# Second norm, third norm and keys of a two-layer cross-attention kernel: the turning of 22 tiles moved from TensorE to DMA block moves and a VectorE 32x32 transpose

## Chip, cores and metric

The kernel runs on one core of a Trainium2 chip, as a single launch. The metric is device microseconds of that core from one launch, the median over several runs. Three runs of the kernel before are known: 907.7, 908.37 and 908.4 us, median 908.37 us. The profile is of one execution and counts from the first to the last instruction of the program; its span is 907.1 us.

The engines are named as the profile names them: PE (TensorE, matrix products), PEld (its weight loads), DVE (VectorE), ACT (ScalarE), POOL (GpSimd) and SP (SyncE, which here only issues DMAs).

## What is computed

Eight batches of a 128x512 token tile `x` go through two layers. Each layer is a gated cross-attention and then a gated dense layer, each on a layernorm of `x` and each added to `x`:

```python
x = x + tanh(g_xattn[0]) * L0_xattn(layernorm(x), ctx, mask, ...)   # 32 heads of 128
x = x + tanh(g_ffn[0])   * L0_ffn(layernorm(x), ...)                # 512x512, dequantized
x = x + tanh(g_xattn[1]) * L1_xattn(layernorm(x), ctx, ...)         # one head of 512
x = x + tanh(g_ffn[1])   * L1_ffn(layernorm(x), ...)                # dense, router, LoRA experts
```

The later stages, which the change touches, are the last three lines. `L1_xattn` is

```python
features_n = rmsnorm(features, fn_w)
Q = rmsnorm(text @ Wq.T + bq, qn_w)
K = rmsnorm(features_n @ Wk.T + bk, kn_w)
attended = softmax(Q @ K.T / sqrt(512)) @ features_n
```

## The kernel before

The first 780 us or so compute the first attention, with 32 heads. They are not touched. What follows are the later stages, for the eight batches `b` = 0 to 7, each a tile with 128 tokens on the partitions and 512 features along the free dimension. A product over features needs the features on the partitions, so each tile that enters a product is turned first.

The later stages are generators, one for each batch and kind of work:

- `ffn0(b)`: layernorm "h1", then the dense product `psf` (12 matmuls of 512 columns), added to `x` by DVE at L777. POOL has added the bias to `x` before that (L1172), so L777 waits for POOL too.
- `keys(b)`: DVE writes `k` (L1196, two halves), ACT squares it for the norm (L1182), POOL makes the inverse root (L421, L426), ACT scales it (L1208), PE turns it (L1127, tile `tpk`), DVE multiplies it by the norm weights into `kT` (L1211).
- `xattn1(b)`: layernorm "h2", the product `psq` (12 matmuls), `q` (DVE, L1233), its norm, the turn of `q` on PE (`tpq`), the scores `s` (four matmuls, eight rows of 128 columns in the trace, L1243), the softmax, a turn of the probabilities (`tpp`), and the product `av` added to `x` at L777.
- `ffn1(b)`: layernorm "h3", the product `o` in two halves of 328 columns (12 matmuls each), the router on DVE, the LoRA turn `thw`, the product `lb`, and the store to `out`.

All three layernorms are `layernorm(b, name)`. ACT makes minus the mean (L1143) and subtracts it (L1150). After a `yield`, `transposed()` turns the result with four 128x128 PE transposes into one PSUM tile `tph` (L1127). `parts_of()` then calls `split()`: ACT rounds the turned tile to the upper part of an fp32r pair (L169) and DVE subtracts that for the lower part (L170). ACT squares `x` for the variance (L1157) and POOL makes the inverse root. Every product is three matmuls for each block of 128 features (`product`, L178, L179, L182): high x high, high x low of the right side, low of the left side x high. So the third matmul of a product, some 0.46 us after the first, is the first that reads the lower part.

`pipeline(starts)` orders the work: in each of its steps, newly started generators advance first, then the older ones, each up to its next `yield`. `starts` gives the step in which each begins: `ffn0(b)` in step 1+b, `keys(b)` in step 4+b, `xattn1(b)` in step 9+b, `ffn1(b)` in step 17+b. Only PE is held to that order (`in_order(*ORD)`, with `ORD` the PE alone). For the other engines and for SP a scheduler decides the order when the program is built; on the chip each engine then takes its instructions strictly in that order and waits for each in turn.

Tiles live in a fixed number of buffers for each tag (`TAGS`): "page" 14, "raw" 7, "moved" 2, "pT" 2, "wo" 8. PSUM banks: "mm" 3 (for `psf`, `psq`, `av`, `o`, `lb`), "sc" 2, "av" 3.

The same detour that the change uses stands already in the first attention: `store_probs` writes the probabilities to DRAM (L725), `move_probs` reads them back in four DMAs so that the 32-row blocks change places (L732), and `transpose_probs` turns all 32x32 blocks with one DVE instruction (L741).

Of the kernel before, what the change touches and what calls it, by code (L numbers as in the profile page):

```python
# [8 lines left out]
F32 = mybir.dt.float32  # L9
# [18 lines left out]
Q32 = 32  # L28
NQ = P // Q32
# [10 lines left out]
OUT_LAG = 6  # L40
FIRST = 6
SHORT = 12
QUAD = 4
AHEAD = 3
WARMING = 7
# [21 lines left out]
def kernel(  # L67
# [37 lines left out]
    nc = tc.nc  # L105
# [3 lines left out]
    dram = ctx.enter_context(tc.tile_pool(name="dram", bufs=2, space=bass.MemoryType.DRAM))  # L109
# [13 lines left out]
    def wide_row(tag, name, dtype=F32):  # L123
        return slot([P, D], tag, name, dtype)
# [4 lines left out]
    def wide(t):  # L129

        return t.bitcast(F32)
# [36 lines left out]
    def split(high, low, src, low_engine=None):  # L168
        mark("high", nc.scalar.copy(high, src))  # L169
        mark("low", (low_engine or nc.vector).tensor_tensor(low, src, wide(high), ALU.subtract))  # L170
# [226 lines left out]
    xs = [keep([P, D], f"x{b}") for b in range(NB)]  # L397
# [31 lines left out]
    def over_free(w, n=P):  # L429

        return w.unsqueeze(2).to_broadcast([P, NDC, n])
# [201 lines left out]
    def by_block(t):  # L633

        return t.rearrange("p b (n k) -> p n b k", k=Q32)
# [315 lines left out]
    rows = []  # L951
# [170 lines left out]
    qkn = keep([P, NDC], "qkn")  # L1122
    def transposed(b, name, src):
        tag = "sc" if b % 2 and name in SC_NAMES else "av"
        tp = ptile([P, NDC, P], tag, f"tp{name}_{b}")
        for dc in range(NDC):
            nc.tensor.transpose(tp[:, dc, :], src[:, bass.ts(dc, P)], ident)  # L1127
        return tp

    def work(b, name, tag, shape=(P, D), dtype=F32):  # L1130
        return slot(list(shape), tag, f"{name}_{b}", dtype)

    def parts_of(b, name, src):

        t = work(b, name, "page", (P, NDC, 2, P), F32R)
        split(t[:, :, 0, :], t[:, :, 1, :], src)
        return t

    def layernorm(b, name, gate=None):


        negm = col(f"nm{name}", b)
        nc.scalar.mul(negm, col(f"sum{name}", b), -1.0 / D)  # L1143
        t = work(b, name, "wo")
        src, dst = xs[b], t
        if name == "h1":

            dst = t.rearrange("p (jj a r) -> p r a jj", jj=NDC, a=2)
            src = src.rearrange("p (r a jj) -> p r a jj", a=2, jj=NDC)
        nc.scalar.activation(dst, src, AF.Identity, bias=negm)  # L1150
        yield
        tp = transposed(b, name, t)
        if name == "h3" and b > 2:
            turns.pop(b - 3)()
        hT = parts_of(b, f"{name}T", tp)
        ss = col(f"ss{name}", b)
        nc.scalar.activation(  # L1157
            work(b, f"junk{name}", "raw"), xs[b], AF.Square, bias=negm, accum_out=ss
        )
        r = col(f"r{name}", b)  # L1160
        inverse_root(r, ss, 1e-5)
        rg = r
        if gate is not None:
            rg = col(f"rg{name}", b)
            nc.gpsimd.tensor_tensor(rg, r, gate, ALU.mult)
        yield
        return hT, r, rg
# [9 lines left out]
        return ps  # L1177

    def inverse_rms(b, name, src):
        junk = work(b, f"junk{name}", "raw")  # L1180
        ss = col(f"ss{name}", b)
        mark("rms", nc.scalar.activation(junk, src, AF.Square, accum_out=ss))  # L1182
        r = col(f"ir{name}", b)
        inverse_root(r, ss, 1e-6)
        return r

    kTs = [page([P, NDC, HALF, P], f"kT{i}", F32) for i in range(2)]
    fns = {}

    def keys(b):  # L1190
        half, j = divmod(b, HALF)
        k = work(b, "k", "v")
# [12 lines left out]
        r2 = inverse_rms(b, "k", k)  # L1205
        yield
        with behind("high"):
            nc.scalar.activation(k, k, AF.Copy, scale=r2)  # L1208
        yield
        tp = transposed(b, "k", k)  # L1210
        nc.vector.tensor_tensor(kTs[half][:, :, j, :], tp, over_free(qkn), ALU.mult)  # L1211
        yield

    def values(b):
# [168 lines left out]
    def ffn1_weights():  # L1383
        for dc in range(NDC):
            t = page([P, 2, 2, NS], f"bw{dc}")
            nc.sync.dma_start(out=wide(t).rearrange("p a h n -> p a (h n)"), in_=bw_kept[:, dc])
            for half in range(2):
                bw[dc, half] = [t[:, part, half] for part in range(2)]
        t = page([P, 2, D], "lora")
        nc.sync.dma_start(out=wide(t), in_=lora_kept)  # L1390
# [13 lines left out]
        nc.vector.tensor_scalar_mul(twice, twice, 2.0)  # L1404
        yield

    def ending():
# [38 lines left out]
        yield  # L1446

    key, ffn, att, last = ([s(b) for b in range(NB)] for s in (keys, ffn0, xattn1, ffn1))

    starts = [[ending()], ffn[:1], ffn[1:2], ffn[2:3], [ffn[3], key[0]]]  # L1450
    starts += [[ffn[b], key[b - 3]] for b in range(4, NB)]
    starts += [[att[0], key[5]], [att[1], key[6]], [att[2], key[7]]] + [[c] for c in att[3:] + last]
    starts[6].append(query_weights())
    starts[13].append(ffn1_weights())
    with in_order(*ORD):
        pipeline(starts)

# [71 lines left out]
```

## Time and profile before

| what | value |
|---|---|
| runs | 907.7, 908.37, 908.4 us |
| span of the profiled execution | 907.1 us |
| PE busy | 900.8 us (99%) |
| DVE busy | 673.1 us (74%) |
| ACT busy | 503.0 us (55%) |
| POOL busy | 460.3 us (51%) |
| granted TensorE clock, 40 slices | full in all of them |
| first product of `ffn0`, first of `psq`, first of `o` | 786.2, 820.5, 858.8 us |
| last PE turn of an "h3" tile | 890.2 us |

The profiled execution's own time on the clock of the runs is not listed beside its span; the three runs lie 0.6 to 1.3 us above the span, which is what lies before its first and after its last instruction.

How to read the profile: a group is a source line, engine and operation, `out<-in` by the program's names with buffer numbers left out, so `tph` stands for the turned tiles of all three norms. "Idle before" is time in which that engine waited, with what ended the wait. In a timeline the columns are the start, the duration, and the instruction; matmuls overlap, so what PE can deliver is read from start to start: 0.23 us for 512 columns, 0.11 us for a 128x128 transpose. A DMA row has the queue's issue time in the timeline, and its time to landing in the DMA view.

### The profile page before, as it was taken

To read this page: it belongs to the slowest core of one execution; us is meant where nothing else is said; L and a number is where in the kernel's file an instruction comes from. 1 tells how busy PE (TensorE), PEld (TensorE's weight loads), DVE (VectorE), ACT (ScalarE), POOL (GpSimd) and SP (SyncE) were. 2 spreads that over 40 slices of the span, in tenths; PEclk is the share of its full clock that TensorE was granted. 3 is DMA by queue.
4 is the path that set the end of the run, shared out by engine and by line. 5 is a ranking of instruction groups with operands and counts; after the bars stand their busy time and mean duration, and the time that the engine had idled before them with its cause. 6 is when DMAs were issued, how large, how long until landed. Compare 5 with 4: busy or idle time off the path is not lost.

```text
span 907.1 us, 16427 instructions
## 1 busy us (share of the span) xinstructions
PE 900.8 (99%) x5381; PEld 799.2 (88%) x5381; DVE 673.1 (74%) x1353; ACT 503.0 (55%) x1426; POOL 460.3 (51%) x513
## 2 busy tenths in 40 slices
PE   9999999999999999999999999999999999999998
PEld 7888888888888899999999999999999998888897
DVE  7888878789889866777677667666686877565587
ACT  6666555667555545545536445453454544588862
POOL 2355534114322436756747657583866844265441
PEclk9999999999999999999999999999999999999999
DMA  7755477889875956667574765766767566814001
GB/s 256 255 162 163 152 205 232 294 280 285 275 238 204 298 196 186 182 193 221 163 238 151 203 215 153 222 176 201 215 165 208 180 178 177 306 47 143 1 24 71
DMA packets 125223, 174.99 MB, mean 193 GB/s; under 512 B 17105, under 2 KB 54737, under 8 KB 124113
## 3 DMA queue, kind: packets, MB, share of 16 engines
q1 hardware_dynamic: 124992, 173.68, 61.5%
q8 instruction: 42, 0.69, 0.3%
q14 instruction: 45, 0.36, 0.1%
q10 hardware_dynamic: 144, 0.26, 0.1%
HBM read 109.86 MB, written 64.03 MB: 192 GB/s over the span
## 4 chain that ended last, share of the span: by engine, by line
PE 93%; DVE 3%; DMA 2%; ACT 1%; issue 0%; POOL 0%; SPq 0%; DVEq 0%; ACTq 0%; POOLq 0%
PE c_v L178 7%; PE c_v L179 6%; PE c_v L182 6%; PE pso L182 6%; PE pso L178 6%; PE pso L179 6%; PE sc L692 6%; PE av L756 6%; PE c_q L178 6%; PE c_q L179 6%; PE c_q L182 6%; PE c_k L178 4%; PE c_k L179 4%; PE c_k L182 4%; PE tph L1127 1%; DMA cxraw<-in_cxT_dram 1%
## 5 line engine op out<-in xcount | busy, mean ns | idle before, releaser
L709 ACT ACTIVATE s<-s,nm 128x128 f32<-128x128 f32 x256 | 99.8, 392 | 78.8 <-DVE nm L699 54.8
L777 DVE SCALAR_TENSOR_TENSOR x<-pso,tg,x 128x512 f32<-128x512 f32 x128 | 93.4, 741 | 52.2 <-PE pso L182 51.3
L717 POOL TENSOR_TENSOR s<-s,rs 128x512 f32<-128x512 f32 x64 | 66.7, 1042 | 111.1 <-DVE rs L715 63.2
L178 PE MATMUL pso<-wo_h,a 128*128 128x512 f32 x256 | 101.9, 411 | 0.0
L179 PE MATMUL pso<-wo_l,a 128*128 128x512 f32 x256 | 101.5, 397 | 0.0
L182 PE MATMUL pso<-wo_h,a 128*128 128x512 f32 x256 | 101.0, 395 | 0.1
L178 PE MATMUL c_v<-wvP,cxT 128*128 128x256 f32 x288 | 84.8, 294 | 0.2 <-ACT v L253 0.2
L182 PE MATMUL c_v<-wvP,cxT 128*128 128x256 f32 x288 | 81.4, 283 | 0.0
L179 PE MATMUL c_v<-wvP,cxT 128*128 128x256 f32 x288 | 81.4, 283 | 0.0
L757 ACT CAST a<-av 128x512 fp32r<-128x512 f32 x64 | 37.4, 584 | 74.4 <-PE av L756 74.0
L679 POOL TENSOR_TENSOR s<-mneg,bias 128x512 f32<-128x512 bf16 x64 | 75.9, 1186 | 0.1
L756 PE MATMUL av<-pT,v 128*128 128x128 f32 x512 | 71.2, 274 | 0.0
L756 PEld LDWEIGHTS av<-pT,v 128*128 128x128 f32 x512 | 67.1, 191 | 2.8
L692 PE MATMUL sc<-k,q 128*128 128x128 f32 x464 | 65.8, 274 | 0.0
L692 PEld LDWEIGHTS sc<-k,q 128*128 128x128 f32 x464 | 61.9, 191 | 3.2
L178 PE MATMUL c_v<-wvP,cxB 128*128 128x256 f32 x216 | 62.1, 289 | 0.0
L758 DVE TENSOR_TENSOR a<-av,a 128x512 fp32r<-128x512 f32 x64 | 43.4, 679 | 24.9 <-ACT a L757 24.5
L179 PE MATMUL c_v<-wvP,cxB 128*128 128x256 f32 x216 | 61.2, 283 | 0.0
L182 PE MATMUL c_v<-wvP,cxB 128*128 128x256 f32 x216 | 61.1, 283 | 0.0
L170 POOL TENSOR_TENSOR wo_l<-raw_wo,wo_h 128x512 fp32r<-128x512 f32 x32 | 41.4, 1293 | 33.8 <-ACT wo_h L169 33.8
L182 PEld LDWEIGHTS pso<-wo_h,a 128*128 128x128 f32 x256 | 48.2, 188 | 10.8 <-DVE a L758 1.3
L695 DVE TENSOR_TENSOR s<-sc,s 128x512 f32<-128x512 f32 x64 | 43.7, 683 | 17.1 <-PE sc L692 12.4
(277 smaller groups left out, 2808.4 us busy)
## 6 DMA issues: line engine op xcount, KB each, us to landing
keys<-keys SPq DMA_DIRECT2D x64, 256.0 KB, 3.5
queries<-queries SPq DMA_DIRECT2D x64, 256.0 KB, 3.5
through<-s SPq DMA_DIRECT2D x64, 256.0 KB, 2.6
moved<-through SPq DMA_DIRECT2D x256, 64.0 KB, 3.0
q<-queries SPq DMA_DIRECT2D x58, 256.0 KB, 3.8
k<-keys SPq DMA_DIRECT2D x58, 256.0 KB, 4.3
raw_wq<-in_wq_dram SPq DMA_DIRECT2D x32, 256.0 KB, 3.9
raw_wv<-in_wv_dram SPq DMA_DIRECT2D x32, 256.0 KB, 4.9
```

The lines of the kernel that those rows point to most:

```text
L170: mark("low", (low_engine or nc.vector).tensor_tensor(low, src, wide(high), ALU.subtract))
L178: nc.tensor.matmul(out, lhsT=lh, rhs=rh, start=first, stop=False, **more)
L179: nc.tensor.matmul(out, lhsT=lh, rhs=rl, start=False, stop=False, **more)
L182: nc.tensor.matmul(out, lhsT=ll, rhs=rh, start=False, stop=last, **more),
L679: nc.gpsimd.tensor_tensor(s, mneg[:, half], bias.unsqueeze(2).to_broadcast([P, NQ, HALF, Q32]), ALU.add)
L692: nc.tensor.matmul(ps[:, j, :], lhsT=q[:, cols], rhs=k[:, cols], start=True, stop=True)
L695: nc.vector.tensor_tensor(s, by_block(ps), s, ALU.add)
L709: e = nc.scalar.activation(one, one, AF.Exp, bias=nm[:, j : j + 1], accum_out=sm[:, j : j + 1])
L717: mark(f"norm{u}", nc.gpsimd.tensor_tensor(s, s, factors, ALU.mult))
L756: nc.tensor.matmul(av[:, b, :], lhsT=v[:, cols], rhs=pT[:, b, :], start=True, stop=True)
L758: mark("al", nc.vector.tensor_tensor(al, av, wide(ah), ALU.subtract))
L777: "x", nc.vector.scalar_tensor_tensor(xs[b], ps, factor, xs[b], ALU.mult, ALU.add, **out)
```

## The change

For the second norm ("h2", all eight batches), the third ("h3", batches 2 to 7) and the keys (all eight), the four PE transposes go: 22 tiles. In their place:

- ACT writes the normed tile in another order of its columns (`by_rows`), so that each quarter of a row has the pieces of all four feature blocks.
- `send()` issues one DMA that stores the tile to DRAM and four that read it back with 32-row blocks exchanged, all on SP's queue.
- `turned()` is one DVE transpose of 32x32 blocks, SBUF to SBUF.
- For these norms `split()` gets POOL for the lower part instead of DVE, and the multiplication of the keys by the norm weights goes from DVE to POOL as well.
- `xattn1(b)` begins two steps earlier, and "h2" waits two steps more between `send` and `turned`; the keys wait one step more. "h3" has no step more.
- The tile that takes the unused squares is one for all (`junk`) instead of one of "raw" for each.
- The loads of the weights of `ffn1` begin two steps later, and are issued only after the last `send` before them.

```diff
+    def send(b, name, t, tag):
+        through = dram.tile([P, NQ, NDC * Q32], F32, tag="rows", name=f"rows_{name}_{b}", bufs=6)
+        nc.sync.dma_start(out=through, in_=t.rearrange("p (n f) -> p n f", n=NQ))
+        moved = work(b, f"{name}moved", tag, (P, NQ, NDC, Q32))
+        blocks = through.rearrange("(i q) n f -> n q i f", q=Q32)
+        for j in range(NQ):
+            move = nc.sync.dma_start(
+                out=moved[bass.ts(j, Q32)].rearrange("p i b k -> p i (b k)"), in_=blocks[j]
+            )
+        mark("sent", move)
+        return moved
+    def turned(b, name, moved, tag):
+        t = work(b, f"{name}turned", tag, (P, NDC, P))
+        nc.vector.transpose(by_block(t), moved)
+        return t
...
+        far = name == "h2" or (name == "h3" and b >= FAR)
...
         nc.scalar.activation(dst, src, AF.Identity, bias=negm)
-        yield
-        tp = transposed(b, name, t)
+        if far:
+            moved = send(b, name, t, "raw")
+        yield
+        for _ in range(2 * (name == "h2")):
+            yield
+        if far:
+            tp = turned(b, name, moved, "raw")
+        else:
+            tp = transposed(b, name, t)
...
-        hT = parts_of(b, f"{name}T", tp)
+        hT = parts_of(b, f"{name}T", tp, nc.gpsimd if far else None)
...
-            nc.scalar.activation(k, k, AF.Copy, scale=r2)
-        yield
-        tp = transposed(b, "k", k)
-        nc.vector.tensor_tensor(kTs[half][:, :, j, :], tp, over_free(qkn), ALU.mult)
+            nc.scalar.activation(
+                by_rows(rows), k.rearrange("p (dc n k) -> p dc n k", n=NQ, dc=NDC), AF.Copy, scale=r2
+            )
+        moved = send(b, "k", rows, "moved")
+        yield
+        yield
+        t = turned(b, "k", moved, "pT")
+        nc.gpsimd.tensor_tensor(kTs[half][:, :, j, :], t, over_free(qkn), ALU.mult)
...
-    starts += [[att[0], key[5]], [att[1], key[6]], [att[2], key[7]]] + [[c] for c in att[3:] + last]
+    starts += [[key[b]] for b in range(5, NB)] + [[] for _ in range(5)] + [[c] for c in last]
+    for b in range(NB):
+        starts[7 + b].insert(0, att[b])
     starts[6].append(query_weights())
-    starts[13].append(ffn1_weights())
+    starts[15].append(ffn1_weights())
```

More of the change, by code (lines that the diff above doesn't have):

```diff
@@ L42 @@
 SHORT = 12
+FAR = 2
 QUAD = 4
@@ L1131, in work, with parts_of, by_rows @@
         return slot(list(shape), tag, f"{name}_{b}", dtype)
-    def parts_of(b, name, src):
+    def parts_of(b, name, src, low_engine=None):
         t = work(b, name, "page", (P, NDC, 2, P), F32R)
-        split(t[:, :, 0, :], t[:, :, 1, :], src)
+        split(t[:, :, 0, :], t[:, :, 1, :], src, low_engine)
+        return t
+    junk = wide_row("kq", "junk")
+    def by_rows(t):
+        return t.rearrange("p (n dc k) -> p dc n k", n=NQ, dc=NDC)
+    def send(b, name, t, tag):
[12 more added lines that the diff above has]
+        nc.vector.transpose(by_block(t), moved)
         return t
@@ L1149, in layernorm @@
             src = src.rearrange("p (r a jj) -> p r a jj", a=2, jj=NDC)
+        far = name == "h2" or (name == "h3" and b >= FAR)
+        if far:
+            dst = by_rows(t)
+            src = src.rearrange("p (dc n k) -> p dc n k", n=NQ, dc=NDC)
         nc.scalar.activation(dst, src, AF.Identity, bias=negm)
+        if far:
+            moved = send(b, name, t, "raw")
         yield
-        tp = transposed(b, name, t)
+        for _ in range(2 * (name == "h2")):
+            yield
+        if far:
+            tp = turned(b, name, moved, "raw")
+        else:
+            tp = transposed(b, name, t)
         if name == "h3" and b > 2:
             turns.pop(b - 3)()
-        hT = parts_of(b, f"{name}T", tp)
+        hT = parts_of(b, f"{name}T", tp, nc.gpsimd if far else None)
         ss = col(f"ss{name}", b)
         nc.scalar.activation(
-            work(b, f"junk{name}", "raw"), xs[b], AF.Square, bias=negm, accum_out=ss
+            junk, xs[b], AF.Square, bias=negm, accum_out=ss
         )
@@ L1179, in inverse_rms @@
     def inverse_rms(b, name, src):
-        junk = work(b, f"junk{name}", "raw")
         ss = col(f"ss{name}", b)
@@ L1206, in keys @@
         yield
+        rows = work(b, "krows", "v")
         with behind("high"):
-            nc.scalar.activation(k, k, AF.Copy, scale=r2)
+            nc.scalar.activation(
+                by_rows(rows), k.rearrange("p (dc n k) -> p dc n k", n=NQ, dc=NDC), AF.Copy, scale=r2
+            )
+        moved = send(b, "k", rows, "moved")
         yield
-        tp = transposed(b, "k", k)
-        nc.vector.tensor_tensor(kTs[half][:, :, j, :], tp, over_free(qkn), ALU.mult)
+        yield
+        t = turned(b, "k", moved, "pT")
+        nc.gpsimd.tensor_tensor(kTs[half][:, :, j, :], t, over_free(qkn), ALU.mult)
         yield
@@ L1385, in ffn1_weights @@
             t = page([P, 2, 2, NS], f"bw{dc}")
-            nc.sync.dma_start(out=wide(t).rearrange("p a h n -> p a (h n)"), in_=bw_kept[:, dc])
+            with behind("sent"):
+                nc.sync.dma_start(out=wide(t).rearrange("p a h n -> p a (h n)"), in_=bw_kept[:, dc])
             for half in range(2):
@@ L1389, in ffn1_weights @@
         t = page([P, 2, D], "lora")
-        nc.sync.dma_start(out=wide(t), in_=lora_kept)
+        with behind("sent"):
+            nc.sync.dma_start(out=wide(t), in_=lora_kept)
         lora.extend(t[:, part] for part in range(2))
```

## Prediction

> **What bounds the kernel.** First the page's busy shares and its chain of work that ended last:
>
> ```profile
> PE 900.8 (99%) x5381; PEld 799.2 (88%) x5381; DVE 673.1 (74%) x1353; ACT 503.0 (55%) x1426; POOL 460.3 (51%) x513
> PE 93%; DVE 3%; DMA 2%; ACT 1%; issue 0%; POOL 0%; SPq 0%; DVEq 0%; ACTq 0%; POOLq 0%
> ```
>
> PE is the path, and the waits of PE after 765 us add up to 0.2 us. So what leaves PE counts fully, and so does any wait that PE gets. The chain in order of time shows one step of the stage that the change meets first:
>
> ```profile
> 816.24 0.44 PE tpk L1127 x4
> 816.68 0.44 PE tph L1127 x4
> 817.12 0.23 PE psf L178
> ...
> 819.88 0.44 PE tpk L1127 x4
> ```
>
> A step is 3.64 us: two turns and twelve matmuls (2.85 us). Next, who else is near full in it. The windows give POOL 18.02 us of the 20 from 800 to 820, and POOL's timeline shows one whole cycle without a gap over 0.1 us:
>
> ```profile
> 810.25 0.19 POOL L1165 TENSOR_TENSOR cols<-cols,tg 128x1 f32<-128x1 f32 x1
> 810.52 0.19 POOL L421 TENSOR_SCALAR cols<-cols 128x1 f32<-128x1 f32 x1
> 810.79 0.55 POOL L426 TENSOR_TENSOR cols<-cols,neghalf 128x1 f32<-128x1 f32 x1
> 811.42 0.50 POOL L421 TENSOR_SCALAR cols<-cols 128x1 f32<-128x1 f32 x1
> 812.00 0.55 POOL L426 TENSOR_TENSOR cols<-cols,neghalf 128x1 f32<-128x1 f32 x1
> 812.52 1.43 POOL L1172 TENSOR_TENSOR x<-x,bias 128x256 f32<-128x256 f32 x2
> ```
>
> The cycle ends at 813.91: 3.66 us; the shortest (803.61 to 807.02) is 3.41. I take 3.45. POOL just keeps up with a PE step of 3.65, not with a shorter one.
>
> **What goes.** From start to start, a turned key takes PE 0.43 to 0.44 us, a turned "h2" 0.35 or 0.36, a turned "h3" 0.44 (the first 0.35): 8 x 0.435 + 8 x 0.355 + 2.55 = 8.9 us. Nothing hides it: **−8.9**. If nothing else changed, 908.4 would become 899.5.
>
> **What comes.** 22 DVE transposes (0.65 from start to start, L741) for 22 DVE instructions of 0.68 that move to POOL: DVE is even. POOL gets 14 lower parts at 1.29 (L170, `wo_l`) and 8 key products at 1.04 (L336, a 128x512 product with a broadcast column): 26 us more, 18 of them before the last `psq`. SP gets 22 x 5 = 110 DMAs. What one costs:
>
> ```profile
> 738.17 0.32 SPq L725 DMA_DIRECT2D through<-s  x1
> 738.59 1.82 SPq L732 DMA_DIRECT2D moved<-through  x4
> ...
> moved<-through SPq DMA_DIRECT2D x44, 64.0 KB, 2.2
> out_dram<-x SPq DMA_DIRECT2D x7, 256.0 KB, 2.0
> ```
>
> Four moves hold the queue 1.82 us, 0.455 each; a store lands 2.0 us after its issue, a move 2.2. So one tile costs SP 2.25 us, and a batch's key and "h2" together 4.5, against PE steps of 3.2 to 4.2.
>
> The order in which the changed program lists each engine's instructions decides the rest, since each engine takes its list strictly. I work with batch numbers and put durations from the rows on that list.
>
> *psf_7.* Without the key, a PE step is 0.355 + 2.845 = 3.20; the turn of batch 2 starts at 796.04 as before, so psf_6 would end at 815.25 (the last matmul drains till 815.45). POOL starts its first cycle at about 799 (the square of key 0, 1 us earlier than before); the bias of batch 6 is the fifth cycle's: 799.0 + 4 x 3.45 + 3.2 = 816.0. DVE before took the lower part of `h1T` of batch 7 ahead of that batch 6 addition:
>
> ```profile
> 816.06 0.68 DVE L170 TENSOR_TENSOR h1T<-tph,h1T 128x512 fp32r<-128x512 f32 x1
> 817.65 0.75 DVE L777 SCALAR_TENSOR_TENSOR x<-psf,cols,x 128x512 f32<-128x512 f32 x1 [0.91 <-POOL x L1172]
> ```
>
> In the changed list it stands behind it: x_6 (816.0, pitch 0.67), the transpose of key 0 (0.65), k_6 (0.80), then this lower part (0.68): 818.8. The upper part on ACT waits likewise for x_6 by way of the mean in front of it. psf_7's third matmul wants it at 815.25 + 0.46: **+3.1**. psf_7 ends 821.2.
>
> *SP's queue.* The first move (key 0) stands behind the store of key 2, which ACT makes ready at 810.5. From 811.0 on, 75 DMAs up to the last of "h2" cost 34 us, and five reads stand close behind the store that they read, 0.4 to 1.7 us of waiting each. The keys' blocks land at 814.6, 819, 822.3, 828.0, 832.1, 837.8, 843.4, 849.2, and h2_7 at 853. DVE's list has a key's transpose ahead of what PE needs, so these landings become PE's:
>
> *psq_0.* DVE: transpose of key 2 at 822.35, x_7 0.65, k_7 0.80, transpose of h2_0 0.65 = 825.1; ACT's upper part (0.6) 825.7; POOL's lower part (1.3) 827.05. PE wants it at 821.2 + 0.46: **+5.4**.
> *psq_1.* Key 3 landed 828.0; two transposes, ACT, POOL: 831.25 against 829.9: **+1.35**.
> *psq_2.* DVE: q_1, which needs psq_1 (ends 833.65), then key 5 (landed 837.8), then h2_2: 839.1. ACT 839.7. POOL has key 5's product (1.12) and 0.55 of small work in front: low at 841.6. Wanted: 833.65 + 0.44 (turn of q_0) + 0.46. **+7.05**.
> *psq_4.* Key 7 (849.2) stands ahead of the softmax maximum and of h2_4: DVE 851.0, ACT 851.6; POOL has key 7's product and two roots first: 854.55 against 850.0: **+4.55**. psq_3, 5, 6 and 7 find their tiles ready.
>
> *h3.* The detour must fit between x_b and `o` of batch b, two steps later. Unhidden it is 2.0 + 0.1 + 1.4 (three issues) + 2.2 = 5.7 us to the last landing: x_4 before is at 869.16, its norm done at 871.43, landed 877.2; DVE comes to the transpose about 878.7, so the transfers are hidden. What follows is not. For batches 2, 4 and 6 the transpose stands on DVE behind the sum or the router's exponential of an `o` that has only just ended. From that end (batch 4): addition 0.2 to 0.85, transpose to 1.5, ACT to 2.15, POOL to 3.5; PE fills 1.5 (`lb`, `tpp`, `av`, `thw`) and 0.3 more: **+1.7**, and by like sums 1.6 and 1.65. Batches 3, 5 and 7 have an `o` half more in between (1.84) and just fit. Together **+5**.
>
> **The sum.** Waits 3.1 + 5.4 + 1.35 + 7.05 + 4.55 + 5 = 26.45; less 8.9 is 17.5. The span would be 924.6; the median of the runs, 1.3 above the span before, 925.9. I say **926**.
>
> **Where the trace has no row.** (a) The key product and the lower part on POOL with the new operands: 1.04 to 1.34 are the ends of like rows. (b) A store of 32-column pieces on ACT: 0.72 (L1150 late, L1208) or 1.24 (the same line in "h1"'s order); 128x128 in pieces of 32 takes 0.39 (L709), so 0.72; at 1.24 ACT would be later by 0.5 a step, on top. (c) SP's pitch: 0.32 (single issues) to 0.48; at 0.32 the landings come up to 10 us sooner and the waits fall to those of rival 1.
>
> [...]
>
> (d) What PE does after idling: at the start of this trace its 512-column matmuls come 0.42 to 0.59 apart until 6.65 us and 0.23 after, though PE has worked since 1.38, so a cold stretch may last 5.3 us and lose half. The two longest waits leave PE without any matmul for 4 and 5 us. Bounds: 0 (nothing after 7 us shows it) and 2 x 2.65 = 5.3. I take 0, since the granted clock is full in every slice.
>
> [...]
>
> **Rivals.**
> 1. *SP keeps up* (pitch 0.32, or the reads find their stores landed). The order of DVE and POOL remains: psf_7 3.1; psq_0 3.8 (x_7, k_7, transpose, ACT, POOL behind psf_7); psq_2 5.8 (POOL has q_1's root and two key products first); "h3" 5. 17.7 − 8.9 = +8.8: **917**; 912 if half the "h3" waits go too. For it: DMA is 0% to 4% busy from 840 to 880. Against: the 1.82 above.
> 2. *Faster.* The tiles are always there before PE; then −8.9: **899.5**. It needs all waits together under 8.9, and POOL's cycle under 3.2 us. For it: "h2" has two steps more, and DVE is no busier. Against: POOL's gapless cycles, and each third matmul now depends on a POOL instruction nearly twice as long as DVE's.
> 3. *The clock falls in the waits*: up to 5.3 more, **931**.
>
> Chances: forecast 0.56, rival 1 0.21, rival 3 0.12, rival 2 0.08, in between about no change 0.03. A measurement of this kernel can tell 0.2% (1.8 us) from no change. Faster 0.08, within 0.2% 0.03, slower 0.89. The range reaches from rival 1 with half its "h3" waits to rival 3 with some 3 us of SP's pitch: **912 to 934**; the forecast's own is 920 to 932.
>
> **What would show it.** Right: PE waits of over 3 us in front of psf_7, psq_0, psq_2 and psq_4, ended by POOL's lower parts; DVE waiting for the keys' moves; SP issuing without a pause from about 811 to 851; the last `psf` before, no wait. Wrong: PE without gaps from 815 to 860; POOL idle between 820 and 845; "h3" waits under 0.5 us. If the waits of PE come to under 9 us, the sign is wrong.

## The result, and the profile after

The changed kernel takes **938.4 us** (median of four runs, 935.4 to 943.9) against 908.2: ratio 1.034, 95% interval 1.031 to 1.037. The forecast was 926, its range 912 to 934. The sign is right, the size is not: 30.2 us more where 17.7 were forecast.

The profiled execution took 935.43 us and has a span of 933.7, 26.6 above that of before. The busy line and the shares of the chain, from the page of the changed kernel:

```profile
PE 903.6 (97%) x5293; PEld 794.9 (85%) x5293; DVE 679.6 (73%) x1353; ACT 504.5 (54%) x1426; POOL 486.2 (52%) x535
...
PE 89%; DVE 3%; DMA 2%; ACT 2%; POOL 2%; SPq 1%; issue 1%; DVEq 0%; ACTq 0%
```

PE has 88 matmul instructions fewer (22 turns of four) and yet is busy for 2.8 us *longer*. So some instructions on it became slower. Its waits from 780 us on, from the view of waits (us in total, times, longest):

```profile
PE psq L179 <- ACT h2T L170: 9.3, 3, 5.0
PE psf L179 <- ACT h1T L170: 3.7, 1, 3.7
PE o L183 <- POOL h3T L171: 3.4, 4, 1.6
PE psq L183 <- POOL h2T L171: 3.3, 4, 1.3
PE o L179 <- ACT h3T L170: 2.8, 3, 1.7
PE psf L183 <- DVE h1T L171: 1.0, 1, 1.0
```

They add up to 23.5. The span grew by 26.6 with 8.9 of turns gone: 35.5 are to be explained, and 12.0 of them are not waits. (The two traces reach the first `psf` at 786.22 and 784.88 us; counted from there, both numbers are 1.3 larger.) PE's timeline shows where they are (start, duration, in brackets the idle time ahead):

```profile
817.72 0.80 PE L179 MATMUL psf<-wf,h1T 128*128 128x512 f32 x1 [3.69 <-ACT h1T L170]
818.31 0.63 PE L180 MATMUL psf<-wf,h1T 128*128 128x512 f32 x1
819.99 0.80 PE L183 MATMUL psf<-wf,h1T 128*128 128x512 f32 x1 [1.05 <-DVE h1T L171]
820.58 0.63 PE L179 MATMUL psf<-wf,h1T 128*128 128x512 f32 x1
821.01 0.63 PE L180 MATMUL psf<-wf,h1T 128*128 128x512 f32 x1
```

Behind the wait the matmuls start 0.43 apart, not 0.23. The windows of the same stretch, PE alone, cut at steps of 3.41 us (us, PE busy and its instructions, granted clock, DMA share, GB/s):

```profile
810.18:813.59 3.41, 3.41 (x18) 1.00 0.52 164
813.59:817.00 3.41, 0.44 (x2) 1.00 0.67 198
817.00:820.42 3.42, 1.65 (x3) 0.50 0.48 135
820.42:823.83 3.41, 3.41 (x9) 0.50 0.57 178
823.83:827.24 3.41, 0.50 (x2) 1.00 0.95 234
827.24:830.66 3.42, 3.29 (x7) 0.50 1.03 359
830.66:834.07 3.41, 1.99 (x9) 1.00 0.61 180
...
837.48:840.90 3.42, 0.40 (x4) 1.00 0.51 165
840.90:844.31 3.41, 1.22 (x2) 0.50 0.65 221
844.31:847.72 3.41, 2.52 (x6) 0.50 0.50 136
847.72:851.14 3.42, 3.42 (x13) 0.50 0.41 135
851.14:854.55 3.41, 3.41 (x20) 1.00 0.37 123
```

Read the busy time and the clock one line further down: a stretch with PE busy for 0.44 is followed by half clock, 1.65 leaves it there, 3.41 restores it. The edges of the clock lie on this grid for the whole stage, a last one from 915.99 to 919.40 (19 steps after 851.14) as well. Four spells, of 6.8, 3.4, 10.2 and 3.4 us, make 23.9 us of half clock, in 5.0 of which PE was idle anyway: **about 9.5 us lost**. The rest is mostly the start after each wait: there are 16 waits, and behind each it takes 0.34 to 0.60 to the next matmul at a wide tile, where the steady step is 0.23 or, at half clock, 0.43.

The profiled run is the shortest of the four, 3.0 under the median. The longest (943.89) has a mean granted clock of 0.980 against 0.987, which makes 18.8 us of clock missing against 12.1. How much of that fell into waits, and so what made it longer, is not known.

How the forecast wait in front of psf_7 came about is seen on ACT and DVE, from their timelines:

```profile
816.99 0.20 ACT L1169 ACTIVATE cols<-cols 128x1 f32<-128x1 f32 x1 [1.22 <-DVE x L778]
817.10 0.57 ACT L170 CAST h1T<-tph 128x512 fp32r<-128x512 f32 x1
```

```profile
816.19 0.75 DVE L778 SCALAR_TENSOR_TENSOR x<-psf,cols,x 128x512 f32<-128x512 f32 x1 [2.09 <-POOL x L1209]
...
816.87 0.71 DVE L1162 STREAM_TRANSPOSE kturned<-kmoved 128x512 f32<-128x512 f32 x1
817.50 1.83 DVE L1232 SCALAR_TENSOR_TENSOR k<-v,rcs,bk 128x256 f32<-128x256 f32 x2
819.26 0.68 DVE L171 TENSOR_TENSOR h1T<-tph,h1T 128x512 fp32r<-128x512 f32 x1
```

The lower part, which before ran ahead of x_6, stands behind x_6, a turned key and a key, and the cast on ACT behind the mean of x_6. SP's moves start at 810.45 and those of the last "h2" at 853.53, near the forecast 811 and 851, but not without a pause: in front of five groups of moves SP stands still for 0.8 to 2.2 us, 8.7 in all. One landing was missed by far. The transfers issued from 822 to 826 (KB, us to landing):

```profile
fn<-w_fn SPq DMA_DIRECT2D x1, 1024.0 KB, 6.0
rows_k<-krows SPq DMA_DIRECT2D x2, 256.0 KB, 2.2
rows_h<-h SPq DMA_DIRECT2D x1, 256.0 KB, 6.2
kmoved<-rows_k SPq DMA_DIRECT2D x3, 64.0 KB, 5.9
```

Moves land in 1.9 to 2.0 (medians) elsewhere. These went out behind a load of 1 MB on SP's queue, which took 6.0 to land while the DMA engines were 0.95 to 1.03 busy (823.83 to 830.66 above), and VectorE waited 4.97 for them.

The traces differ by up to 2.0 us before any of the changed work begins, so hours of different traces, and of the forecast, are compared from here on as counted from the start of the first `psf` (786.22 in the kernel before, 784.88 here). So counted, keys 0 to 2 landed within 1 us of the forecast. Key 3's transpose was forecast at 41.8 and ran at 46.6, and those of keys 5 to 7 came 4.4 to 4.6 late. The third matmuls of psq_1, psq_2 and psq_4 came 5.0, 4.9 and 4.5 late. GpSimd, whose idling between 820 and 845 the prediction named as a sign of being wrong, waited there three times, for 2.82, 3.76 and 2.25 us; the first two of these:

```profile
827.27 1.28 POOL L171 TENSOR_TENSOR h2T<-h2turned,h2T 128x512 fp32r<-128x512 f32 x1 [2.82 <-ACT h2T L170]
832.30 1.04 POOL L1252 TENSOR_TENSOR kT<-kturned,qkn 128x512 f32<-128x512 f32 x1 [3.76 <-DVE kturned L1162]
```

### The profile page after: what moved, and what is told of

The parts are those of the page before. It is cut to its first block, busy times and chain, and to the rows that moved or that the text cites. A ratio compares the mean times of both kernels' runs of the same rounds, so it can differ in the third digit from the quotient of the medians.

```text
span 933.7 us, 16471 instructions
## 1 busy us (share of the span) xinstructions
PE 903.6 (97%) x5293; PEld 794.9 (85%) x5293; DVE 679.6 (73%) x1353; ACT 504.5 (54%) x1426; POOL 486.2 (52%) x535
## 4 chain that ended last, share of the span: by engine, by line
PE 89%; DVE 3%; DMA 2%; ACT 2%; POOL 2%; SPq 1%; issue 1%; DVEq 0%; ACTq 0%
PE c_v L179 6%; PE c_v L183 6%; PE c_v L180 6%; PE pso L183 6%; PE pso L179 6%; PE pso L180 6%; PE sc L693 6%; PE av L757 6%; PE c_q L179 5%; PE c_q L183 5%; PE c_q L180 5%; PE c_k L179 5%; PE c_k L183 5%; PE c_k L180 5%; SPq L1153 1%; DMA kmoved<-rows_k 1%
## 5 line engine op out<-in xcount | busy, mean ns | idle before, releaser
L179 PEld LDWEIGHTS c_v<-wvP,cxT 128*128 128x128 f32 x288 | 54.8, 190 | 1.7 <-ACT v L254 0.6
```

Of the source, the lines that this page charges most:

```text
L179: nc.tensor.matmul(out, lhsT=lh, rhs=rh, start=first, stop=False, **more)
```

## Experiments

Times are medians beside the kernel before on the same chip (908.1 to 908.6 in all of them); the ratio's interval is in brackets. The theory was by now: turns −8.9, waits +23.5, clock and restarts +12. Its rivals were that the clock's share is only cover for later landings, that SP's issues alone or the lists alone make the waits, or that GpSimd does.

### 1. Fillers in the waits, whole change

```diff
+    def fill(name, w, n):
+        spare = ptile([P, D], "sc", f"fill_{name}")
+        for _ in range(n):
+            nc.tensor.matmul(spare, lhsT=w[:, :P], rhs=w[:, :D], start=True, stop=True)
...
+        if b in (0, 1, 2):
+            fill(f"q{b}", wq1_p[0][0], (12, 20, 16)[b])
         ps = dense(b, "q", hT, wq1_p)
```

> The changed kernel with 70 more matmuls that nothing reads (128x512, written to a spare PSUM tile) standing in TensorE's list where it waits: 14 ahead of psf_7, 12, 20 and 16 ahead of psq_0, psq_1 and psq_2, 8 ahead of the last o. At 0.2325 us each they take 16.3 us that TensorE waited anyway. Clock theory (of the 35.5 us that the changed profile lies above 907.1 - 8.9, 23.5 are waits and 12.0 are matmuls run at a granted clock of 0.5, and each of the two stands on its own): the granted clock stays 1.00 after 800 us and the time falls by the whole 12, to about 926. Cover theory (the clock falls, but the transfers of the next tile would have held TensorE nearly as long): the clock stays 1.00, the waits grow by 7 to 10, and the time falls by 2 to 5 only, to 933 to 936. If the clock falls in spite of the matmuls, or the clock has no part in it, the time stays or rises by what the fillers overshoot.

**942.2** [1.036, 1.039]. The clock stayed at 1.00 through psf_7, psq_0 and psq_1, until 845.5, and nothing came of it. Counted from the first `psf`, psq_0 began at 40.8 (42.4 in the changed kernel), so 1.5 us sooner, but psq_1 at 49.1 (48.6) and psq_2 at 59.9 (58.0). Ahead of psq_1 stands key 3, whose turn waits for its moves. The first `psf` and that turn, in the changed kernel and then with fillers:

```profile
784.88 0.48 PE L179 MATMUL psf<-wf,h1T 128*128 128x512 f32 x1
831.51 0.71 DVE L1162 STREAM_TRANSPOSE kturned<-kmoved 128x512 f32<-128x512 f32 x1 [4.97 <-DMA kmoved<-rows_k]
...
786.55 0.48 PE L179 MATMUL psf<-wf,h1T 128*128 128x512 f32 x1
832.99 0.71 DVE L1168 STREAM_TRANSPOSE kturned<-kmoved 128x512 f32<-128x512 f32 x1 [6.29 <-DMA kmoved<-rows_k]
```

That is 46.6 and 46.4 us after the first `psf`. So what set the start of psq_1 was this landing, and not how fast the product before ran. The cover theory foresaw that the gain would be covered; that the time would rise above 938 it did not foresee. The fillers ahead of psq_1 overshot by some 0.5 us, and the store of key 5 was read only 4.2 us after its issue (2.2 before). Both moved in one run, so this experiment does not price the clock.

### 2. The third norm alone, without and with fillers

The first run has only "h3" of batches 2 to 7 by transfers; the second adds this:

```diff
+FILL = {2: 9, 4: 9, 6: 18}
...
                 ps = ptile([P, NS], "mm", f"o{i}_{b}")
+                for _ in range(FILL.get(b, 0) * (i == 1)):
+                    nc.tensor.matmul(ps, lhsT=lora[0][:, :P], rhs=lora[0][:, :NS], start=True, stop=True, ...)
```

> Only the third norm of batches 2 to 7 turned by transfers; keys and second norm by TensorE. TensorE is rid of 6 x 0.44 = 2.6 us. In the changed profile this stage waits 6.2 us and loses about 1.6 to a half clock in the last batch. No other kind's transfers lie in this stretch, so both theories say the same: -2.6 + 6.2, and up to 1.6 more: 911 to 914. If the time is under 908 the waits of this stage came from the delays before it.

> The run with only the third norm by transfers, and 36 matmuls that nothing reads (128x328, 0.15 us each, written where the following real matmul starts afresh): 9 ahead of o of batches 2 and 4, 18 ahead of that of batch 6, 5.4 us in all, less than the 6.6 us that TensorE waits there. In the run without them the excess is -2.6 + 6.6 of waits + about 6.3 in which 13.6 us ran at a granted clock of 0.5. Clock theory (each stretch of the 3.41 us grid with TensorE busy under half of it puts the next one at half clock, which costs as much as the wait itself): the fillers keep every stretch above half, the clock stays 1.00, and the time falls by 5 to 6.5, to 912 to 913.5. Rival (the matmuls that look slow are held by their inputs): no change, 917 to 920.

**918.5** [1.009, 1.012] and **914.2** [1.005, 1.008]. The first lies 4.5 above its range: the clock fell in three places, not in one. Here no landing stands behind a wait, and the clock shows its price. Windows of the run without fillers, PE alone, columns as above:

```profile
867.32:870.73 3.41, 1.78 (x10) 1.00 0.30 81
870.73:874.15 3.42, 3.42 (x14) 0.51 0.21 77
...
880.97:884.39 3.42, 1.65 (x9) 1.00 0.45 144
884.39:887.80 3.41, 3.41 (x14) 0.50 0.23 87
...
894.63:898.04 3.41, 1.15 (x6) 1.00 0.26 79
898.04:901.45 3.41, 2.48 (x9) 0.51 0.26 93
901.45:904.87 3.42, 3.42 (x14) 0.50 0.00 0
```

And the same places with fillers:

```profile
867.32:870.73 3.41, 2.90 (x18) 1.00 0.29 81
884.39:887.80 3.41, 3.41 (x22) 1.00 0.39 131
```

36 matmuls that nothing reads save 4.3 us. Waits that remain (1.6) and fillers (5.4) make 7.0 against 6.6 of waits, so the clock is worth about 4.7 here, somewhat less than expected. No single wait in these stretches is longer than 1.62; two in one stretch are enough. The waits came where the forecast had put them, batches 2, 4 and 6: 1.63, 1.77 and 3.19, the last twice its forecast.

### 3. No transfers at all, and the other two kinds alone

```diff
-        through = dram.tile(...)
-        nc.sync.dma_start(out=through, in_=t...)
...
-        return moved
+        return t.rearrange("p (n dc k) -> p n dc k", n=NQ, dc=NDC)
```

> The changed kernel without its 88 transfers in the late stages: VectorE's transpose reads the tile where it lies, so 32-row blocks are not exchanged and the output is another one; the order of all other work is left to the same rules. Theory of the prediction (SP's queue and the landings make 8 to 9 us of the waits, the lists of VectorE, ScalarE and GpSimd the rest, near 17): 915 to 922, with waits in front of psf_7 and the h3 stage left and at most one spell of half clock. Rival (the transfers are nearly the whole loss): below 903. Rival (the transfers cost nothing, the lists all): above 932.

> Only the keys turned by transfers; the second and third norm by TensorE, att[0] to att[7] started as in the kernel before. TensorE is rid of 8 x 0.435 = 3.5 us. Theory now (three kinds of tiles share SP's queue, and one tile's moves stand behind another's landing, so most of the loss is in their meeting): alone the keys cost SP 18 us of the 40 it has, nothing that TensorE needs soon stands behind a landing, the waits are 2 to 6 us and the time 906 to 911. Rival (each kind costs its own: the keys' landings stand in VectorE's list ahead of what TensorE wants, whoever else uses the queue): about half of the whole +30, 918 or more.

> Only the second norm's tiles turned by transfers (two steps of lead, lower parts on GpSimd, as in the changed kernel); keys and third norm by TensorE. TensorE is rid of 8 x 0.355 = 2.8 us. Theory now (the loss is in the meeting of the kinds on SP's queue and in VectorE's list): landings come 4 to 6 us after the store, two steps of 3.6 cover them, 905 to 912. Rival (each its own): 915 or more, TensorE waiting in front of psq_0 to psq_4 for the lower parts and the transposes. If the three parts' excesses over 908.2 add up to the 30 of the changed kernel, nothing is lost in their meeting; if they make under 15, most is.

**913.3** [1.004, 1.007] without transfers; **916.4** [1.008, 1.011] keys alone; **911.1** [1.002, 1.004] second norm alone. Without transfers 25.1 of the 30.2 are gone, more than its theory had (915 to 922). But this is not the price of the transfers alone, since the scheduler listed the other work anew too (the loads of `ffn1`'s weights, for one, have no `send` left to stand behind). From VectorE's timeline of that run:

```profile
813.53 0.65 DVE L171 TENSOR_TENSOR h1T<-tph,h1T 128x512 fp32r<-128x512 f32 x1
815.03 0.75 DVE L778 SCALAR_TENSOR_TENSOR x<-psf,cols,x 128x512 f32<-128x512 f32 x1 [0.85 <-POOL x L1200]
```

The lower part of `h1T` of batch 7 stands ahead of x_6 again, as in the kernel before, and no wait is left before psf_7, where the changed kernel has 4.74. PE's 10.1 us of waits in this run stand elsewhere, in front of `psq`, `tpq` and `thw`, and not where its theory had them (psf_7 and "h3"). So transfers and lists are not separated by it.

The excesses of the kinds alone are 8.3 (keys), 3.0 (second norm) and 10.4 (third norm), 21.7 together: 8.5 arise only where the kinds stand together. The keys' rival ("918 or more") and theory ("906 to 911") both missed; the second norm came within its theory's range. The run with keys alone has the wait before psf_7 (3.44 and 1.14) in full, with no other kind near it.

### 4. Easing the transfers

Four edits of the whole change: stores issued by ScalarE; one transfer of 256 KB in place of the four moves; three of the four 1 MB loads left out; the three edits together.

```diff
-        nc.sync.dma_start(out=through, in_=t...)
+        nc.scalar.dma_start(out=through, in_=t...)
...
-        for j in range(NQ):
-            move = nc.sync.dma_start(out=moved[bass.ts(j, Q32)]..., in_=blocks[j])
+        move = nc.sync.dma_start(out=moved..., in_=through...)
...
-        if b % 2 == 0:
+        if b == 0:
             fns[b], fns[b + 1] = load_page(...)
+        elif b % 2 == 0:
+            fns[b], fns[b + 1] = fns[0], fns[1]
```

> The changed kernel with the 22 stores issued by ScalarE, right behind the instruction that writes the tile, and the moves on SP as before. Queue theory (a store stands in SP's queue behind moves that wait for an earlier store's landing, and its own moves wait a whole landing more): SP is rid of 22 x 0.42 us and of the order; landings come 3 to 6 us sooner and the time falls to 922 to 932, less what ScalarE loses to the issues. Rival (VectorE's list and the round trip of about 5 us decide, not the queue): within 3 us of 938, or above it where ScalarE's casts come later.

> The changed kernel with one transfer in place of the four moves of a tile: the whole 256 KB back in its own order, so blocks are not exchanged and the output is another one; the store, the round trip through DRAM, the bytes and the lists' rules stay. SP issues two transfers a tile and not five. Issue theory (SP's 2.25 us a tile is what makes the landings late): SP needs 0.9, and of the 25.1 us that lie between the changed kernel (938.4) and the one without transfers (913.3) more than half goes: 916 to 926. Rival (the round trip itself, 4 to 5 us from store to landing, and the order in SP's queue are the loss): 932 to 938. One transfer of 256 KB may land later than four small ones, which would hide part of the gain.

> The changed kernel with only the first of the four 1 MB loads of the last product's weights, the other batches using its rows (another output). Load theory (the DMA engines, 0.65 to 1.0 busy from 820 to 830, carry the 1 MB ahead of key 3's moves, which land at 831.3 instead of 827.4; psq_1 stands behind them in VectorE's list): the moves land in about 2, the wait before psq_1 (2.05) goes, what follows comes 2 to 3 us sooner and the time falls to 934 to 936.5. Rival (the next landing in SP's order holds it as long): 937 to 939.

> The changed kernel with the stores issued by ScalarE, one transfer of the whole tile for its four moves (blocks not exchanged) and only the first of the 1 MB loads. Alone the first gave 5.4 us and the second 4.7. Additive theory (queue order, number of issues and the load each hold their own stretch): 10 to 13 us together, 925 to 928. Rival (each relieves the same wait): 930 to 933. Either way what is left up to the 913.3 of the run without transfers is the round trip through DRAM itself, store and move one after the other, and the lists laid out for it.

**933.0** [1.026, 1.029], **933.7** [1.026, 1.029], **931.6** [1.024, 1.028], together **928.9** [1.021, 1.024]. Each is worth 4.7 to 6.8, the three 9.5 and not 17: they relieve one another's stretches. The four runs of the changed kernel spread over 8.5 us, so the order among the three is not shown. Only the single transfer fell where one of its two ranges was, its rival's; the others lie up to 2.4 us beside theirs. SP's pitch, the heart of the forecast, gives 4.7: with two issues a tile SP is idle most of the time, and psq_0 still begins 42.2 us after the first `psf` (42.4 in the changed kernel).

Without the load the moves issued from 820 to 830 land in 1.9 (median), key 3 is turned at 39.1 and not at 46.6, the wait before psq_1 is gone as expected, and the third matmul of psq_4 comes at 67.9, where the forecast had 68.3 and the changed kernel 72.9. But in this run, too, the lists are others: the wait before psf_7 falls from 4.74 to 0.64 and the one before psq_0 rises from 2.92 to 8.30, so the 6.8 us are not shown to be the load's alone. With all three edits the wait before psf_7 is gone entirely. Of the 25.1 us, 15.6 stay when queue, issues and load are eased. They are the round trip (store 3.4 to 3.7 us, then move 2.9, the medians from 820 to 830 of this run), lists laid out for it, and the other lists of the run without transfers; these were not separated.

### 5. Lower parts on VectorE, and one order put right

```diff
-        hT = parts_of(b, f"{name}T", tp, nc.gpsimd if far else None)
+        hT = parts_of(b, f"{name}T", tp, None)
```

```diff
-        add_to_x(b, ps, rg, "h2")
+        with behind("low"):
+            add_to_x(b, ps, rg, "h2")
```

> The lower parts of the tiles turned by transfers on VectorE (0.68 us each) and not on GpSimd (1.28). In the changed profile 7 us of TensorE's waits end with GpSimd's lower parts. GpSimd theory (that engine, saturated to 824 us and slower per instruction, holds them): these waits go to under 2 and the time falls to 930 to 934. Rival (VectorE's list, where a lower part then stands behind transposes that wait for landings, gives it back): 937 to 945, with the waits ended by VectorE.

> The changed kernel with one order put right: the addition of psf to x stands behind the lower part of the next tile of the first norm on VectorE, so that neither x_6 nor its mean on ScalarE stands ahead of the two parts that psf_7 wants. Order theory (TensorE waited 4.74 us in front of and in psf_7 for parts that were held by x_6's chain through GpSimd): the wait falls to about 2 (the square of x_0 and one turned key still stand ahead). If what follows is not itself held by a landing, the time falls by 2.7, and by up to 3.4 more where the half clock behind it goes: 932 to 936. Landing theory (the next tiles come no sooner, so TensorE waits later what it does not wait here): 937 to 939, with the wait before psq_0 longer by as much.

**933.1** [1.026, 1.031] and **940.4** [1.034, 1.037]. GpSimd's lower parts cost about 5, as its theory had it; but the waits that end with lower parts of turned tiles fall from 6.7 to 4.5 and not to under 2. The order alone gains nothing: the wait before psf_7 falls from 4.74 to 2.27, as expected, and that before psq_0 rises from 2.92 to 4.80. From that run's timelines:

```profile
786.11 0.48 PE L179 MATMUL psf<-wf,h1T 128*128 128x512 f32 x1
...
817.54 0.50 PE L179 MATMUL psf<-wf,h1T 128*128 128x512 f32 x1 [2.27 <-ACT h1T L170]
...
827.21 0.80 PE L179 MATMUL psq<-wq,h2T 128*128 128x512 f32 x1 [4.80 <-ACT h2T L170]
...
832.58 0.71 DVE L1162 STREAM_TRANSPOSE kturned<-kmoved 128x512 f32<-128x512 f32 x1 [6.07 <-DMA kmoved<-rows_k]
```

Counted from the first `psf`, psq_0 begins at 41.1, 1.3 us sooner than in the changed kernel. Key 3 is turned at 46.5 (46.6), and psq_1 begins at 48.5 (48.6). The order theory for the whole loss is refuted: what came sooner is lost before psq_1, which the landing of key 3 holds. Why this run ends later than the changed kernel is not shown.

### 6. Versions that give the transfers room

Keys alone, begun two steps later and three steps from store to turn, with seven buffers for their tiles in place of two; second norm alone with lower parts on VectorE; both kinds, only in the batches with room; then keys alone with the lists put right, and the same with three tiles of the second norm. The decisive edits of the keys' versions (the third `yield`, the buffers and the place of a key's first operation are left out here):

```diff
-        starts[7 + b].insert(0, att[b])
+        starts[9 + b].insert(0, att[b])
+        starts[6 + b].append(key[b])
...
+        with behind("low"):
             t = turned(b, "k", moved, "pT")
...
+        with behind("low"):
             nc.vector.scalar_tensor_tensor(q, ps, rh, bq, ALU.mult, ALU.add)
+        with behind("high"):
             r = inverse_rms(b, "q", q)
```

> Only the keys by transfers, but each begun two steps later and with one step more between store and turn, so that no key's work lies beside psf_0 to psf_4, and only three keys' beside the rest of that stage. Theory (GpSimd's cycle of 3.45 us with a key in it cannot follow a psf step of 3.2, and VectorE's list has two turned keys ahead of the lower part that psf_7 wants): the waits of 4.6 us around psf_7 and the half clock behind them go; 8 x 0.435 less TensorE work remain: 904.5 to 908. Rival (the landings are what TensorE waits for, wherever they are put): 912 or more.

> Only the second norm by transfers, with the lower parts on VectorE. With them on GpSimd TensorE waited 2.9 us for lower parts, 0.7 for an upper part, and one stretch of 3.4 us ran at half clock. GpSimd theory (it is full through the last psf, and a lower part of 1.28 us stands behind a bias and two roots): those 2.9 and the half clock (1.7) go, and the time falls from 911.1 to 906 to 908, under the kernel before for the first time. Rival (the transposes' landings, or VectorE's list, hold it): 910 to 913.

> Only those tiles by transfers whose stretch has room: keys of batches 3 to 7 (begun two steps later, three steps from store to turn), second norm of batches 2 to 7 (two steps, lower parts on VectorE); keys 0 to 2, second norm 0 and 1 and the whole third norm by TensorE. TensorE is rid of 5 x 0.435 + 6 x 0.355 = 4.3 us. Theory (where transfers and their followers have room, TensorE is not kept waiting; the waits of the runs with one kind alone lay at psq_0, psq_1 and psq_5): waits of 0 to 1.7 us, no half clock, 904 to 906.5, clear of the kernel before. Rival (two kinds on SP's queue again hold each other up, and VectorE's list puts a turned key ahead of a lower part): 908 or more.

> Keys alone by transfers, begun late as in the run at 907.9, with the lists put right: a turned key, a key's first operation and q stand behind the lower part of the step, q's square behind the upper part. That run waited 1.04 us before psq_1 (its lower part was ready but stood behind x_7, two keys and a turned key) and 0.65 before psq_4 (its upper part stood behind the square of q_3). Order theory: both waits go and the time falls to 905.5 to 907, clear of the kernel before (908.2) by 0.2%. Rival (the waits move on to other places, since VectorE's list is as long as before): 907.5 to 909.

> The same with the second norm's tiles of batches 3, 5 and 7 by transfers too, sent three steps ahead of their turn, lower parts on VectorE: 3 x 0.355 = 1.1 us less TensorE work. Theory (with three steps and every second tile, SP has room and no landing is waited for): 0.5 to 1.1 us under the run with keys alone. Rival (two kinds on SP hold each other up, as in the run at 912.5): 908 or more, with waits in front of the turned tiles.

**907.9** [0.999, 1.001], **908.8** [1.000, 1.001], **912.5** [1.003, 1.006], **906.5** [0.997, 0.999] and **910.0** [1.001, 1.002]. Keys begun late take 8.5 us less than the keys of the change alone (916.4), which is all that these had cost (8.3): the loss was a matter of place and room. The later start, the step more and the buffers came in one edit, so which of them did it is not shown. The second norm with lower parts on VectorE gained 2.3 but missed its range (906 to 908). With keys begun late two waits were left, from the view of waits:

```profile
PE psq L183 <- DVE h2T L171: 1.0, 1, 1.0
PE psq L179 <- ACT h2T L170: 0.7, 1, 0.7
```

With the lists put right that view has no line from 790 on, and the time is 0.2% under the kernel before: the only version that beats both. From its page:

```profile
PE 897.6 (99%) x5349; PEld 795.4 (88%) x5349; DVE 675.2 (75%) x1353; ACT 503.2 (56%) x1426; POOL 468.4 (52%) x521
```

Of the 3.5 us that eight turns weigh, 2.0 arrive in the medians (906.51 against 908.47). Two kinds at once fail again, in both mixtures, though each had room by count. Both rivals had the time right; their reason, that two kinds hold each other up in SP's queue, is not shown. In the last run 1.7 of PE's 2.3 us of waits stand in front of `tpq` and end with VectorE, not in front of a turned tile.

## Why the prediction was wrong, step by step

| step | forecast | changed profile |
|---|---|---|
| 22 turns less | −8.9 | −8.9 (PE had 88 instructions fewer) |
| psf_7 | 3.1 | 4.74 |
| psq_0 | 5.4 | 2.92 |
| psq_1 | 1.35 | 2.05 |
| psq_2 | 7.05 | 6.09 |
| psq_4 (with 0.22 at psq_5) | 4.55 | 1.56 |
| "h3" | 5 | 6.2 |
| all waits | 26.45 | 23.6 |
| half clock and restarts | 0 | 12 |
| turn of key 3, after the first `psf` | 41.8 | 46.6 |

- **The first step that failed is *SP's queue*, with its landings of keys 3 to 7.** It left out the 1 MB load that the same queue issues ahead of key 3's moves. The landing taken for 828.0, or 41.8 us after the first `psf`, let the turn run only at 46.6. psq_1 to psq_4 then came 4.5 to 5.0 late; counted so, the whole span came 10.4 late. In four traces (changed kernel, fillers, one order put right, lower parts on VectorE) key 3 is turned at 46.4 to 46.6 and psq_1 begins at 48.5 to 49.1, whatever the clock or the order ahead of it.
- **The second is (d)**: "I take 0, since the granted clock is full in every slice." A kernel that never idles cannot show what idling costs. The bounds, 0 to 5.3, counted two waits of one cold spell each. In the changed kernel a spell of 3.4 us repeats while the stretches remain broken (busy for 1.22 and 2.52 of 3.41 from 840.90 on), up to three times, and two waits of under 2 us (1.66 and 1.56, in the last `o`) start one too: 12 us, 9.5 of them half clock, in place of 0. It counts after psq_4, where no landing is waited for: there the other 5.9 of the 10.4 us arise, 1.5 in waits above the forecast's and the rest in half clock (an estimated 1.6, in the last `o`) and in starts behind waits.
- That 12 more would make the forecast's own sum 938 is partly luck. The waits were 2.9 under the forecast's, and the profiled run lies 3.0 under the median: 899.5 + 23.5 + 12 gives 935.
- The two prices cannot simply be added in the first part of the stage: fillers kept the clock there and saved nothing. Part of the 12 is therefore cover for landings, and how large a part stays open. In the "h3" part it is shown as loss, 4.7 in the run of that kind alone.
- Rival 3 named the mechanism and priced it at 5.3 at most. It had spells at the two longest waits; there were four, after psf_7 and in the last `o` too.
- The waits were forecast at each place and in sum to 12%, but not each in size: psq_0's is about half of its forecast and psq_4's a third. psq_0's wait is shorter since psf_7, partly at half clock, ended at 824.2 and not at 821.2; its own third matmul came 2.9 late. Most of the waits (15.8 of 23.5) ended with the upper part on ACT, and only 6.7 with GpSimd's lower parts, by which the forecast had most of them end.
- *SP's queue*, its weight: it was taken for the reason of nine of the forecast's us (926 against rival 1's 917). With three fifths of the issues gone the time falls by 4.7; with the loads gone, and other lists, by 6.8.
- *POOL and the lists*: the wait before psf_7 came as described, 4.74 for 3.1. Freed of the lower parts, GpSimd gives back 5.3.
- *h3*: batches 2, 4 and 6 were forecast at 1.6 to 1.7 each. Alone, that kind has 1.63, 1.77 and 3.19; in the changed kernel they are 1.63, 1.11 and 3.22, with 0.28 at batch 3. Why the last is twice as long is not shown.
- Rival 1 has a slip: half of the 5 us of "h3" gone from 917 leaves 914.7, not 912. The range's lower end hangs on it; the result does not.
- Rival 2 ("the tiles are always there") did not happen in the change as made, but was within reach for the keys, with another start and other lists: 906.5.

A spell does not need one long wait: in the run with the third norm alone the stretch 880.97 to 884.39 holds waits of 0.98 and 0.79 and no longer one, PE is busy for 1.65 of it, and half clock followed.

## What to carry to other kernels

Where an engine that sets the time never waits, price a new wait at its length plus the clock that it may lose, and look for stretches, here of 3.41 us, in which the waits together make half (1.77 us of waits were enough in the run with the third norm alone). Taking 0.44 us off that engine pays only if the detour, here by the landings below an estimated 5.4 to 6.0 us of transfers, a transpose and a list position on three engines, is given room before anything asks for its result; one kind of tile, with a step more between store and turn and its place in the lists put right, gained 0.2%, three kinds at once lost 3.4%. When moving transfers into a stretch, list what else its queue carries there: here one load of 1 MB ahead of moves of 64 KB made them land in 5.9 us, where without it they land in 1.9. And when a run leaves something out, look whether the scheduler's order of the rest is still the same.

## What the runs showed of the hardware

- In these traces the granted clock of TensorE changes on a fixed grid of 3.41 us: in the changed kernel the first spell of half clock in the later stages begins at 817.00 and the one in the last `o` ends at 919.40, 30 steps later. In the nineteen profiles of this case, cut along the grid from 750 us on, each of the 38 stretches at full clock with PE busy for 0.48 of it or less was followed by half clock, and none over 0.54; of four in between (0.49 to 0.52), two were. From half clock each stretch busy over 0.90 led back, and none under 0.82; of five in between, three did.
- In the changed kernel a 64 KB move lands in 1.9 to 2.0 us (medians of the three kinds), and in 5.9 behind a load of 1 MB; a 256 KB store in 2.1 (keys) or 2.7 (norms), and in 6.2 there. The single transfer of 256 KB, in its run, lands in 2.8 to 2.9 (medians). Four moves, the last issued 1.4 us after the first, are by these numbers an estimated 3.3, so about 0.4 later than one.
